# Moving four stages of a hand-ordered attention block to other slots

## The chip, the cores and the metric

The kernel runs on one core of one Trainium2 chip. The metric is the time of one execution on the device in microseconds (us). The engines are TensorE (PE, with its weight loads PEld), VectorE (DVE), ScalarE (ACT), GpSimd (POOL) and SyncE (SP), which only issues DMAs here. Each engine works through its own queue in order; semaphores tie the queues together.

## What is computed

The input x is 4 x 4096 x 512 in float32. Three residual steps follow each other: half an FFN, neighbourhood attention, half the same FFN again.

```python
x = x + 0.5 * ffn(layernorm(x))
x = x + attention(layernorm(x))
x = x + 0.5 * ffn(layernorm(x))
```

The FFN is one 512 x 512 product with a bias. Its input and its weight are first quantised in blocks of 32 values to a 6-bit grid, each block with a scale of its own (largest magnitude over 7.5). The attention has 16 heads of 32 features; each query sees 13 neighbouring keys (its window is shifted at the ends of the sequence), gets a bias by relative position, and goes through softmax, the weighted sum of the values, and an output product.

## The kernel before

The 16384 rows are 128 tiles of 128 rows; four tiles are a group. Attention works on items: item m is one group and one of four chunks of 128 features (4 heads), so there are 128 items too. Every float32 operand of a product is split into two float16 parts, high and low, and a product of a tile is 12 matmuls of 128 x 512 (three pairs of parts, four chunks), written by `product` (L144). High parts are made on ACT, low parts on DVE (L193 and L197 for the norms).

The work is cut into stages, Python generators that are hung up on a line of slots by hand. `begin(slot, stage, rank)` hangs a stage up; `run_slot` runs what hangs there, lowest rank first, each up to its next `yield n, rank`, and hangs it up again n slots later. The order in which the program is written down this way is the order on every engine; no scheduler changes it. Seven slots (`STEP`) are one step, and each step takes one tile t and one item m further in every stage. The names below are those of the profile.

- `load` (L169) fetches tile t into x.
- `moments` (L173, L174, DVE) takes mean and variance; `quantised_norms` then makes the quantised input of an FFN, at most two tiles at a time, the first norm of tile t+15 (n1) together with the third norm of tile t (n3): factors rsq, nbq on POOL (L179 to L188), normalise yq on ACT (L226), block maxima sc and their reciprocals on DVE (L232, L233, L237), scale on POOL (L239), round to 8 bits on ACT (L242), scale back on POOL (L244), high and low parts hlq (L193, L197), and a DMA transpose into xT.
- `first_half`: product pmf (f1), sum into x on DVE (L272), the second norm of the tile (rsn, yn, hln), and a transpose into x2.
- `values`: product pmv, copied out by ACT (L307) and DVE (L308), stored to DRAM; `load_stack` brings it back, three shifted copies under each other (vs).
- `project_qk`: two products pmqk (q and k), copied out by ACT (L379) and DVE (L383), q spread over two interleaved copies by ACT (L390).
- `softmax`: small matmuls for the scores ps (L458); on DVE the bias table and the second half of the sums (L500, L503) and the maxima top (L507); POOL subtracts (L509); ACT takes the exponentials (L511); DVE sums and inverts (L514 to L516); POOL multiplies (L518); ACT and POOL make the parts of p (L522, L523, L525); a DMA transposes p into pT (L527).
- `attend`: small matmuls pv (L549; pw for an 18th block of queries), copied to a ring by ACT (L576) and DVE (L582).
- `project_out`: product pmo from the ring, sum into x on DVE (L595), and at once the moments of n3.
- `second_half`: product pmf again (f2), sum into x (L272), store to DRAM (L601).
- `add_bias` adds a bias to x on POOL (L610), three times for each tile.

The slots come from the constants of L607: tile t runs f1 at 7t+5, v at 7t+20, out at 7t+93 and f2 twelve later; item m runs q and k from 7m+38, scores from 7m+42, values at 7m+59. Modulo 7 this gives the order of a step. The last tiles (`LAST`, `HELD`, `out_slot`, `second_slot`) have slots of their own. PSUM has three buffers for all products of a tile (`ps_m`), one for scores and one for values, so a product waits until the one that had its buffer is copied out.

Of the kernel before, what the change touches and what calls it, by code (L numbers as in the profile page):

```python
# [63 lines left out]
def macaron_kernel(  # L64
# [67 lines left out]
    def bc(t, n):  # L132

        return t.unsqueeze(2).to_broadcast([t.shape[0], t.shape[1], n])
# [4 lines left out]
    def product(pm, lhs, rhs):  # L139

        n = 0
        for a, b in ((0, 1), (1, 0), (0, 0)):
            for c in range(KC):
                nc.tensor.matmul(  # L144
                    pm, lhs(a, c), rhs(b, c), start=(n == 0), stop=(n == 3 * KC - 1)
                )
                n += 1
# [7 lines left out]
    def begin(slot, stage, rank=5):  # L155
        slots.setdefault(slot, []).append((rank, stage))
# [159 lines left out]
    def span(j):  # L316

        q0 = min(j * QN, length - QN)
        return q0, min(max(q0 - NS, 0), length - KN)

    def kind(j):
        return 1 if j == 0 else 2 if j == n_blocks - 1 else 0

    def late(j):

        return QR - QN if j == n_blocks - 1 else 0
# [11 lines left out]
    def straight(n):  # L338

        return -(-n // 2)  # L340
# [5 lines left out]
    n_items = n_batch * NG * KC  # L346
    qk, probs, stacks = {}, {}, {}

    def item_of(m):

        g, c = divmod(m, KC)
        return g // NG, g % NG, c
# [88 lines left out]
    def softmax(m):  # L441

        b, g, c = item_of(m)
        j0, j1 = group_blocks[g]
        n = j1 - j0
        tq, tk = qk.pop(m)
        ps = ps_s.tile([P, 2, 2, 2, 256], F32, tag="s", name=f"ps{m}")
        half = straight(n)
        for a in range(half):
            for part, sides in ((0, 2), (1, 1)):  # L450
                for i in range(a, n, half):
                    q0, k0 = (KN + at - g * GT for at in span(j0 + i))
                    q0 -= late(j0 + i)
                    u, w = divmod(a, PSB)
                    for r in (0, 2 * D):
                        rows = slice(r, r + 2 * D)
                        o = r if i < half else 2 * D - r
                        nc.tensor.matmul(  # L458
                            ps[o : o + 2 * D, i // half, u, :sides, w * KN : (w + 1) * KN],
                            tq[rows, part, 2 * q0 : 2 * (q0 + QR)],  # L460
                            tk[rows, :sides, k0 : k0 + KN],
                            start=part == 0, stop=part == 1,
                        )

        yield 1, 9
        sf = sfp.tile([P, MAXB, KN], F32, tag="sf", name=f"sf{m}")

        both = sf[:, : 2 * half, :].rearrange("p (v w) k -> p v w k", v=2)

        def parts(special):  # L470

            for w, e in ((0, PSB), (PSB, half)):
                lone = [(v, x) for v, x in special if w <= x < e]
                for v, x in lone:
                    yield slice(v, v + 1), slice(x, x + 1), 2 + v
                two = min(e, n - half)
                w0 = w + (1 if (0, w) in lone else 0)
                two -= 1 if (1, two - 1) in lone else 0
                if w0 < two:
                    yield slice(0, 2), slice(w0, two), 0  # L480
                for v, x, y in ((0, two, e), (1, w, w0)):
                    y = min(y, (half, n - half)[v])
                    if x < y and not (v == 0 and (v, x) in lone):
                        yield slice(v, v + 1), slice(x, y), v

        def sums(v, w, side):

            u, x = divmod(w.start, PSB)
            t = ps[:, v, u, side, x * KN : (x + w.stop - w.start) * KN]
            return t.rearrange("p v (w k) -> p v w k", k=KN)  # L490

        special = []
        if kind(j0) == 1:
            special.append((0, 0))
        if kind(j1 - 1) == 2:
            special.append((1, n - half - 1))
        for v, w, k in parts(special):
            o = both[:, v, w, :]
            bias = table[:, k : k + v.stop - v.start, c, :].unsqueeze(2).to_broadcast(o.shape)
            nc.vector.tensor_tensor(o, sums(v, w, 0), bias, ALU.add)  # L500
        for v, w, _ in parts([]):
            o = both[:, v, w, :]
            nc.vector.tensor_tensor(o, o, sums(v, w, 1), ALU.add)  # L503
        yield 1, 2
        s = sf[:, :n, :]
        top = sm.tile([P, MAXB], F32, tag="top", name=f"top{m}")
        nc.vector.tensor_reduce(top[:, :n], s, AX.X, ALU.max)  # L507
        yield 1, 4
        nc.gpsimd.tensor_tensor(s, s, bc(top[:, :n], KN), ALU.subtract)  # L509
        yield 1, 9  # L510
        nc.scalar.activation(s, s, AF.Exp, scale=alpha)  # L511
        yield 1, 4
        total = sm.tile([P, MAXB], F32, tag="total", name=f"total{m}")
        nc.vector.tensor_reduce(total[:, :n], s, AX.X, ALU.add)  # L514
        nc.vector.reciprocal(total[:, :n], total[:, :n])
        nc.vector.tensor_tensor(total[:, :n], total[:, :n], p_scale[:, :n], ALU.mult)  # L516
        yield 1, 4
        nc.gpsimd.tensor_tensor(s, s, bc(total[:, :n], KN), ALU.mult)  # L518
        yield 2, 8
        p = p_tile  # L520
        ph = p[:, :n, :KN]
        nc.scalar.copy(ph, s)  # L522
        nc.scalar.copy(p[:, :n, 2 * KN : KV], ph)  # L523
        yield 2, 4
        nc.gpsimd.tensor_tensor(p[:, :n, KN : 2 * KN], s, ph, ALU.subtract)  # L525
        pT = ptp.tile([P, MAXB, P], F16, tag="pT", name=f"pT{m}")
        nc.sync.dma_start_transpose(out=pT[:, :n, :], in_=p[:, :n, :].rearrange("p n k -> p (n k)"))  # L527
        probs[m] = pT
# [58 lines left out]
    def project_out(t, slot):  # L587

        r = t * P % RING
        pm = ps_m.tile([P, dim], F32, tag="mm", name=f"pmo_{t}")  # L590
        product(
            pm, lambda s, c: ring[:, s, c, r : r + P], lambda s, c: wt[:, s, c, PO : PO + dim]
        )
        yield 1, 8
        nc.vector.scalar_tensor_tensor(xs[t], pm, cp, xs[t], ALU.mult, ALU.add)  # L595
        moments(slot, t, "n3")

    def second_half(t):

        yield from ffn(t, "f2")  # L600
        nc.sync.dma_start(out=of[t * P : (t + 1) * P, :], in_=xs.pop(t))  # L601


    EARLY = 3
    STEP = 7

    F1, V, QK, SC, PV, OUT, F2 = 5, 2 * STEP + 6, 5 * STEP + 3, 6 * STEP, 8 * STEP + 3, 13 * STEP + 2, 12  # L607

    def add_bias(t, b):
        nc.gpsimd.tensor_tensor(xs[t], xs[t], b, ALU.add)  # L610
# [8 lines left out]
    HELD = range(NT - 15, NT - 7)  # L619
    LAST = NT - GROUP - 1  # L620

    def out_slot(t):


        i = t - LAST
        if i >= 0:
            return (n_items - 1) * STEP + PV + 3 + 2 * i
        if i >= 1 - GROUP:
            return LAST * STEP + PV + 21 + 4 * i
        return t * STEP + OUT  # L630

    def second_slot(t):

        i = t - LAST
        if t in HELD:
            return (n_items - 1) * STEP + PV - (16, 13, 10, 6, 5, 4, 3, 2)[t - HELD[0]]
        if i in (-2, -1):
            return out_slot(NT - 1) + 3 + i
        return out_slot(t) + F2

    for t in range(NT):
        k = t * STEP
        sooner = (0, 2, 5, STEP)[t] if t <= EARLY else 0
        begin(k - 18 - (STEP if t == EARLY else 0), one(load, t), 0)
        slot = k - 10 - (10 if t == EARLY else 0)
        enlist(slot, t, "n1")
        if not 0 < t < EARLY:
            begin(slot - 1, one(moments, slot, t, "n1"), 1)
        begin(k + F1 - sooner, first_half(t))
        begin(k + V, values(t))  # L650
        begin(k + F1 - sooner, one(add_bias, t, half_ffn_b), 8)
        at = out_slot(t)
        begin(at - 5, one(add_bias, t, after_b), 8)
        enlist(at + 2, t, "n3")
        begin(at, project_out(t, at + 2))
        begin(at + 6 if t < LAST else second_slot(t) - 2, one(add_bias, t, half_ffn_b), 8)
        begin(second_slot(t), second_half(t))
    for slot in together:
        if together[slot][0][0][1] == "n3" or together[slot][0][0][0] >= EARLY:
            begin(slot, quantised_norms(slot), 1)  # L660
    for m in range(n_items):
        k = m * STEP
        begin(k + QK, project_qk(m))
        begin(k + SC, softmax(m), 6)
        begin(k + PV, attend(m), 6)
    for n in range(n_batch * NG):
        k = n * GROUP * STEP
        b, g = divmod(n, NG)
# [4 lines left out]
    with tc.tile_pool(name="setup", bufs=1) as sp, tc.tile_pool(name="scratch", bufs=2) as scr:  # L673
# [23 lines left out]
        for o in chunks:  # L697
            w, i = (qkv_w, o) if o < 3 * KC else (proj_w, o - 3 * KC)
# [145 lines left out]
        for turned in (0, 2):  # L844
            for h in range(4):
                at = row_of(h ^ turned)
# [41 lines left out]
        slot = first  # L888
# [49 lines left out]
```

## Time and profile before

| what | value |
|---|---|
| median of three runs | 2293.57 us (2292.76 to 2294.65) |
| the profiled execution | 2295.28 us, its span 2293.5 us |
| PE busy | 2214.2 us, 97% of the span |
| PE weight loads busy | 1052.9 us, 46% |
| DVE busy | 2011.7 us, 88% |
| POOL busy | 1969.2 us, 86% |
| ACT busy | 1695.5 us, 74% |
| mean granted clock of TensorE | 0.993 |
| chain that ended last: share of PE | 87% |
| chain: share of DVE, ACT, POOL, DMA | 7%, 2%, 2%, 1% |

The span goes from the first instruction's start to the last one's end. A busy time is the sum of an engine's instructions; waiting for a semaphore does not count. The timeline gives for each instruction its start from the beginning of the span, its length, the line of the kernel, and what it writes and reads; in brackets stands idle time of the engine before it and what ended that.

### The profile page before, as it was taken

The numbers are of one execution on the slowest core, as the hardware profiler recorded it, in microseconds if no ns is written. First come the engines' busy times: TensorE is split into PE (matmuls) and PEld (weight loads), VectorE is DVE, ScalarE is ACT, GpSimd is POOL, SyncE is SP. The second block draws the span as 40 slices with busy tenths as digits, with TensorE's granted clock in tenths as the row PEclk, the third lists the DMA queues.
The fourth block names the chain that finished last, engine by engine and source line by source line (L and its number), as shares of the span: only waits on it lengthen the run. The fifth ranks groups of instructions, "written<-read, shape, count | busy, mean of one in ns | idle before, by whom it ended". The sixth has DMA issues, their size and how long they took to land.

```text
span 2293.5 us, 65425 instructions
## 1 busy us (share of the span) xinstructions
PE 2214.2 (97%) x26771; PEld 1052.9 (46%) x26771; DVE 2011.7 (88%) x3769; ACT 1695.5 (74%) x2544; POOL 1969.2 (86%) x2006
## 2 busy tenths in 40 slices
PE   3799999999999999999999999999999999999978
PEld 1344444444444444444444444444444444444433
DVE  6899998888988988898988998888988988989775
ACT  5697777777777777777777777777777777777752
POOL 4588988988988988888888888888888889888776
PEclk9999999999999999999999999999999999999989
DMA  7687776777767777777776776777776777866654
GB/s 201 153 178 161 162 160 154 159 162 158 160 156 155 164 162 154 161 158 157 162 158 155 162 161 154 160 157 155 164 160 151 167 158 154 166 155 147 137 107 104
DMA packets 926213, 359.61 MB, mean 157 GB/s; under 512 B 719452, under 2 KB 890328, under 8 KB 925912
## 3 DMA queue, kind: packets, MB, share of 16 engines
q1 hardware_dynamic: 925568, 354.90, 70.8%
q8 instruction: 209, 3.42, 0.6%
q14 instruction: 92, 0.75, 0.1%
q10 hardware_dynamic: 344, 0.53, 0.1%
HBM read 110.26 MB, written 67.29 MB: 77 GB/s over the span
## 4 chain that ended last, share of the span: by engine, by line
PE 87%; DVE 7%; ACT 2%; POOL 2%; DMA 1%; issue 1%; SPq 0%; ACTq 0%; DVEq 0%; POOLq 0%
PE pmqk L144 27%; PE pmf L144 26%; PE pmo L144 14%; PE pmv L144 13%; PE ps L458 4%; PE pv L549 3%; DVE stn L173 1%; DVE hlq L197 1%; DVE hln L197 1%; DVE sc L232 1%; ACT qk L390 0%; DVE x L272 0%; POOL yq L239 0%; DVE total L514 0%; DVE qf L383 0%
## 5 line engine op out<-in xcount | busy, mean ns | idle before, releaser
L144 PE MATMUL pmf<-wt,xT 128*128 128x512 f16 x3048 | 702.7, 381 | 13.3 <-DMA xT<-hlq 7.4
L144 PE MATMUL pmqk<-x,wt 128*128 128x512 f16 x3072 | 705.8, 379 | 0.4 <-DVE after_b L836 0.4
L144 PEld LDWEIGHTS <-xT 128*128 128x128 f16 x3048 | 298.4, 98 | 377.2 <-DMA xT<-hlq 15.2
L144 PEld LDWEIGHTS <-wt 128*128 128x128 f16 x3072 | 289.7, 98 | 336.0 <-issue 1.3
L239 POOL TENSOR_TENSOR yq<-yq,r 128x1024 f32<-128x1024 f32 (+1 forms) x141 | 247.1, 1752 | 135.6 <-DVE r L237 124.1
L144 PE MATMUL pmv<-wt,x 128*128 128x512 f16 x1536 | 353.9, 380 | 4.2 <-DVE qf L383 2.6
L144 PE MATMUL pmo<-wt,ring 128*128 128x512 f16 x1536 | 357.2, 383 | 0.0
L390 ACT ACTIVATE qk<-qf,parity 128x1024 f16<-128x1024 f16 x256 | 349.3, 1432 | 0.0
L610 POOL TENSOR_TENSOR x<-x,half_ffn_b 128x512 f32<-128x512 f32 x256 | 327.8, 1281 | 0.0
L272 DVE SCALAR_TENSOR_TENSOR x<-pmf,coef,x 128x512 f32<-128x512 f32 x256 | 180.0, 703 | 144.7 <-PE pmf L144 141.1
L576 ACT ACTIVATE ring<-pv 128x510 f16<-128x510 f32 (+7 forms) x176 | 78.7, 475 | 307.3 <-PE pv L549 234.4
L173 DVE BATCH_NORM_STATS2 stn<-x 128x6 f32<-128x512 f32 x384 | 265.2, 691 | 8.8 <-DMA x<-in_L_attn_x_dram 0.2
L244 POOL TENSOR_TENSOR yq<-q,sc 128x1024 f32<-128x1024 fp8e4 (+1 forms) x141 | 246.2, 1746 | 4.8 <-ACT q L242 4.8
L144 PEld LDWEIGHTS <-x 128*128 128x128 f16 x1536 | 150.5, 98 | 186.9 <-issue 4.9
L242 ACT ACTIVATE q<-yq,nudge 128x1024 fp8e4<-128x1024 f32 (+1 forms) x141 | 150.0, 1064 | 115.9 <-POOL yq L239 107.6
L144 PEld LDWEIGHTS <-ring 128*128 128x128 f16 x1536 | 141.2, 98 | 160.5 <-issue 5.0
L518 POOL TENSOR_TENSOR sf<-sf,total 128x714 f32<-128x714 f32 (+2 forms) x128 | 178.7, 1396 | 37.2 <-DVE total L516 19.3
L226 ACT ACTIVATE yq<-x,nbq,rsq 128x512 f32<-128x512 f32 x254 | 193.1, 803 | 16.7 <-POOL nbq L185 15.2
L525 POOL TENSOR_TENSOR p<-sf,p 128x714 f16<-128x714 f32 (+2 forms) x128 | 192.5, 1504 | 0.0
L509 POOL TENSOR_TENSOR sf<-sf,top 128x714 f32<-128x714 f32 (+2 forms) x128 | 182.4, 1425 | 3.5 <-DVE top L507 3.3
L197 DVE TENSOR_TENSOR hlq<-yq,hlq 128x1024 f16<-128x1024 f32 (+1 forms) x141 | 167.6, 1189 | 8.7 <-ACT hlq L193 6.6
L610 POOL TENSOR_TENSOR x<-x,after_b 128x512 f32<-128x512 f32 x128 | 162.9, 1274 | 0.0
(143 smaller groups left out, 3441.0 us busy)
## 6 DMA issues: line engine op xcount, KB each, us to landing
vs<-vd SPq DMA_DIRECT2D x144, 357.0 KB
x<-in_L_attn_x_dram SPq DMA_DIRECT2D x128, 256.0 KB
vd<-vt SPq DMA_DIRECT2D x128, 256.0 KB
out_dram<-x SPq DMA_DIRECT2D x128, 256.0 KB
vs<-vd SPq DMA_DIRECT2D x24, 378.0 KB
vs<-vd SPq DMA_DIRECT2D x24, 315.0 KB
rows<-in_L_attn_qkv_w_dram SPq DMA_DIRECT2D x12, 256.0 KB
xT<-hlq SPq DMA_TRANSPOSE x141
```

Source lines behind the costliest of these rows:

```text
L144: nc.tensor.matmul(pm, lhs(a, c), rhs(b, c), start=(n == 0), stop=(n == 3 * KC - 1))
L173: nc.vector.bn_stats(st, xs[t])
L197: nc.vector.tensor_tensor(hl[:, :, 1, :], y, hl[:, :, 0, :], ALU.subtract)
L226: nc.scalar.activation(y[:, u], xs[t], AF.Identity, bias=nb[:, u : u + 1], scale=rs[:, u : u + 1])
L239: nc.gpsimd.tensor_tensor(yb, yb, bc(r, QB), ALU.mult)
L244: nc.gpsimd.tensor_tensor(yb, q8.rearrange("p u (n q) -> p (u n) q", q=QB), bc(sc, QB), ALU.mult)
L272: nc.vector.scalar_tensor_tensor(xs[t], pm, cf, xs[t], ALU.mult, ALU.add)
L390: nc.scalar.activation(to, whole[0], AF.Copy, scale=parity[:, e : e + 1])
L509: nc.gpsimd.tensor_tensor(s, s, bc(top[:, :n], KN), ALU.subtract)
L518: nc.gpsimd.tensor_tensor(s, s, bc(total[:, :n], KN), ALU.mult)
L525: nc.gpsimd.tensor_tensor(p[:, :n, KN : 2 * KN], s, ph, ALU.subtract)
L610: nc.gpsimd.tensor_tensor(xs[t], xs[t], b, ALU.add)
```

## The change

The constants and ranks move these stages: `attend` four slots later (7m+63, behind the scores of item m+3 in the same slot), except that the last three items keep 7m+59; `project_out` two slots later (7t+95) and the joint norms with it (n1 from 7t-10 to 7t-8 for tiles after `EARLY`, n3 still two slots behind the out-projection); f2 at fourteen slots behind the out-projection and so four later (7t+109); softmax's sums on DVE and all of softmax behind them one slot later. `LAST_PV` keeps the slots of the last tiles' out-projections and second FFNs. In the ranks, out-projection goes behind the second FFN and that behind k in their common slot. No instruction is added or removed.

```diff
@@ softmax
         nc.scalar.activation(s, s, AF.Exp, scale=alpha)
-        yield 1, 4
+        yield 2, 4
         total = sm.tile([P, MAXB], F32, tag="total", name=f"total{m}")
@@
-    F1, V, QK, SC, PV, OUT, F2 = 5, 2 * STEP + 6, 5 * STEP + 3, 6 * STEP, 8 * STEP + 3, 13 * STEP + 2, 12
+    F1, V, QK, SC, PV, OUT, F2 = 5, 2 * STEP + 6, 5 * STEP + 3, 6 * STEP, 9 * STEP, 13 * STEP + 4, 14
+
+    LAST_PV = (n_items - 1) * STEP + 8 * STEP + 3
@@ out_slot
-            return (n_items - 1) * STEP + PV + 3 + 2 * i
+            return LAST_PV + 3 + 2 * i
         if i >= 1 - GROUP:
-            return LAST * STEP + PV + 21 + 4 * i
+            return LAST * STEP + 82 + 4 * i
         return t * STEP + OUT
@@ second_slot
         if t in HELD:
-            return (n_items - 1) * STEP + PV - (16, 13, 10, 6, 5, 4, 3, 2)[t - HELD[0]]
+            return LAST_PV - (16, 13, 10, 6, 5, 4, 3, 2)[t - HELD[0]]
         if i in (-2, -1):
             return out_slot(NT - 1) + 3 + i
-        return out_slot(t) + F2
+        return out_slot(t) + (F2 if t < LAST else 12)
@@
-        slot = k - 10 - (10 if t == EARLY else 0)
+        slot = k - (8 if t > EARLY else 20 if t == EARLY else 10)
@@
-        begin(at, project_out(t, at + 2))
+        begin(at, project_out(t, at + 2), 7)
         begin(at + 6 if t < LAST else second_slot(t) - 2, one(add_bias, t, half_ffn_b), 8)
-        begin(second_slot(t), second_half(t))
+        begin(second_slot(t), second_half(t), 6)
@@
-        begin(k + PV, attend(m), 6)
+        begin(k + (PV if m < n_items - 3 else PV - 4), attend(m), 7)
```

## What was predicted

> **What bounds the kernel now.** I began with the busy shares in 40 slices, to see which engine is full and where.
>
> ```profile
> PE   3799999999999999999999999999999999999978
> DVE  6899998888988988898988998888988988989775
> POOL 4588988988988988888888888888888889888776
> ```
>
> TensorE (PE) is in the top class from the third slice nearly to the end; VectorE (DVE) and GpSimd (POOL) sit at 8 to 9 tenths, so they have 10 to 15% to give away and no more. A table of 100 us stretches says how full PE is; from 300 to 2100 us all eighteen rows read 100.00, as here:
>
> ```profile
> 1000.00:1100.00 100.00, 100.00 (x1242) 47.85 (x1240) 89.57 (x166) 76.58 (x114) 89.22 (x88) 1.00 0.72 157
> ```
>
> The columns after the stretch are its length, then the busy us of PE, weight load, DVE, ScalarE (ACT) and POOL, then the granted clock: PE 100, DVE 89.6, ACT 76.6, POOL 89.2, clock 1.00. Next, the timeline of PE for one step (start, length, what):
>
> ```profile
> 1000.80 0.81 PE L458 MATMUL ps<-qk 64*64 64x84 f16 x68
> 1001.53 2.76 PE L144 MATMUL pmo<-wt,ring 128*128 128x512 f16 x12
> 1004.14 2.75 PE L144 MATMUL pmqk<-x,wt 128*128 128x512 f16 x12
> 1006.82 0.69 PE L549 MATMUL pv<-pT,vs 126*32 126x30 f16 x68
> 1007.45 2.76 PE L144 MATMUL pmqk<-x,wt 128*128 128x512 f16 x12
> 1010.04 2.75 PE L144 MATMUL pmf<-wt,xT 128*128 128x512 f16 x12
> 1012.63 2.75 PE L144 MATMUL pmv<-wt,x 128*128 128x512 f16 x12
> ```
>
> The next scores (ps) start at 1017.91, so a step lasts 17.11 to 17.12 us and PE sets it. A product of 12 matmuls starts 2.59 to 2.60 us after the one ahead when that is a product too (1010.04, 1012.63), but a small block starts 2.68 us after the product ahead of it (1004.14 to 1006.82): entering each small block costs 0.08 to 0.09 us. Everything else hides behind PE as long as it keeps the step.
>
> **What the change does to the queues.** I read the order on each engine from the changed program.
>
> *PE.* The order q, k, second FFN (f2), out-projection, first FFN (f1), v, scores, values replaces f2, scores, out, q, values, k, f1, v. No matmul is added. The values now follow the scores directly, so one of two entries from a product is gone (0.085 us) and one from block to block is new; the trace has none such. Bounds: it costs nothing (0.085 won) or as much as the old entry (0 won). I take the middle, 0.04: both blocks have small tiles, but of different shape. PE's own need becomes 17.04 to 17.12. The Trainium skill ("TensorEngine Tiling (Array Packing)", Key Properties) says that a switch of tiling mode drains TensorE; by that the new entry costs like the old one, and nothing is won.
>
> *DVE.* A step holds the same 24 kinds of operations. Start to start in the timeline of 1000 to 1018 us: q low part L383 0.67, the norms' L173 and L174 three times 0.73+0.10, f2 and f1 sums L272 0.70+0.68, out sum L595 0.76, k low L383 0.66, L197 of hlq 1.12, L514 0.92, L515 0.30, L516 0.10 when nothing is in its way (at 165.15), L308 0.60, L232 1.24, L233 0.23, L237 0.27, L500 0.95, L503 1.05, L582 0.60, L507 0.82, L197 of hln 0.60. Sum 14.8 us. That fits 17.05.
>
> *New waits around PE.* PSUM buffers change hands: the out product now takes the buffer of q, so PE waits for L383 of q. On DVE everything from the out sum round to the next L383 of q stands in front of that wait: 14.8 less the three items between (0.73+0.10+0.70) is 13.2; with 2.79 from the product's start to its sum (the last pmf starts at 1000.49, L272 at 1000.90) the circle is 16.1 us. It closes inside 17.05 with 0.9 to spare. f1 takes the buffer of f2 and v that of out; at PE's pace those sums end 1.7 us before they are needed and nothing stands in front of them on DVE.
>
> *DMAs and SP.* No transfer is added. hlq's transpose had 7.17 us from L197's end (1008.06) to its product (1015.23), and in the steady part no product waited for it; the new order gives 8.2 us at PE's pace and 7.1 at my forecast pace, nothing. Its turn on SP is behind the out store, which waits only for L272 of f2, done four us earlier. The p transpose is issued one slot later and read four later: nothing. The stack loads keep their slots; the last reader of the same buffer moves from 8 slots ahead to 4, some 10 us, so SP is not held. x tiles live four slots longer, of 161 that 23 buffers give: nothing.
>
> *ACT.* It is busy 76.6 of 100; its low rank work moves, and it comes in below as a link.
>
> **Where it goes wrong: POOL and DVE stop each other.** The reader should see this in two places of the old trace.
>
> ```profile
> 202.18 1.42 DVE L197 TENSOR_TENSOR hlq<-yq,hlq 128x1024 f16<-128x1024 f32 x1 [0.25 <-ACT hlq L193]
> 203.53 1.94 DVE L197 TENSOR_TENSOR hln<-yn,hln 128x512 f16<-128x512 f32 x1
> ...
> 201.03 1.49 POOL L525 TENSOR_TENSOR p<-sf,p 128x714 f16<-128x714 f32 x1
> 202.49 2.43 POOL L509 TENSOR_TENSOR sf<-sf,top 128x756 f32<-128x756 f32 x1
> ```
>
> POOL's L509 takes 1.39 to 1.46 us elsewhere. Here it began under DVE's L197 and ended 1.32 us after that one's end (203.60). The L197 of hln, 0.68 us elsewhere, ended 0.55 us after L509. So one waits for the whole of the other. In the steady step it is the same, but cheap:
>
> ```profile
> 1005.48 1.39 POOL L509 TENSOR_TENSOR sf<-sf,top 128x714 f32<-128x714 f32 x1
> ...
> 1006.86 1.20 DVE L197 TENSOR_TENSOR hlq<-yq,hlq 128x1024 f16<-128x1024 f32 x1
> 1007.03 1.08 POOL L179 TENSOR_SCALAR rsq<-mv 128x2 f32<-128x2 f32 x1 [0.16 <-DVE mv L174]
> ...
> 1011.01 1.27 POOL L610 TENSOR_TENSOR x<-x,half_ffn_b 128x512 f32<-128x512 f32 x1
> ...
> 1011.41 0.91 DVE L516 TENSOR_TENSOR total<-total,p_scale 128x17 f32<-128x17 f32 x1
> ```
>
> L179 lasts 0.19 alone (1016.86) and 1.08 under L197; L516 0.18 alone and 0.91 behind L610. Only L197 and L516 show it; L272, L595 and L383, which read PSUM, do not. The Trainium skill ("SBUF — State Buffer", Who interferes with whom) has the rule: a DVE instruction with two SBUF inputs and a GpSimd instruction that reads SBUF exclude each other, and whichever issues second fully blocks. It adds no number to the sum.
>
> Take the new step at PE's pace, q's start as 0. The out sum comes at 7.78+2.79 = 10.57; behind it L173, L174 and L383 of k, so L197 of hlq is asked at 10.57+0.76+0.73+0.10+0.66 = 12.8. On POOL the order is L509, half_ffn_b add, L244, L525, half_ffn_b add, the four small ones of the joint norm, after_b add. The top (L507) would end at about 6.4, and L509 follows: 1.40+1.24+1.87+1.46 later, at 12.4, the second add begins and runs to 13.6. **They collide**: L197 would wait some 0.8. Moreover L197 of hln now follows L507 directly and is asked 0.1 us ahead of L509, so L509 waits 0.5 for it and the add comes at 12.9; then it waits for L197. Either order loses about a microsecond, because a circle runs through both:
>
> L507 0.90, POOL L509 1.40, add 1.24, L244 1.87, L525 1.46, add 1.36 (1.27 and the 0.08 gap ahead of a small one), L179 0.27, L182 0.67, L187 0.28, L188 0.23: 9.68. ACT: two norms L226 0.71+0.80 (they now stand in front of L307, which DVE's L308 needs), L307 0.58: 2.09. DVE: L308 0.60, L232 1.24, L233 0.23, L237 0.27, L500 0.95, L503 1.05, L582 0.60, back to L507: 4.94. Together 16.7, and 0.2 for hand-overs of 0.03 to 0.14 each: **16.9 without blocking**, only 0.15 inside PE's pace. Blocking adds 0.5 at L509 and 0.75 where L179 waits behind L197 (L197 ends 1.08 after the add, less what L179 would have taken): **18.15 us**. In the order before, the small ones of the joint norm followed L509 at once (1005.48, 1007.03), so the circle was shorter by three long POOL operations, 4.6 us, and hlq's L197 met only the small L179.
>
> **Sum.** f2 runs with tiles 0 to 112 in the regular pattern, 113 steps; I take 111, the first two filling. 111 x (18.15 - 17.12) = 114 us. The ramp (nine steps without out and f2, 11 to 14 us long, DVE 97 busy of 100) may lose or win up to 5 us by the same collisions; the end keeps its slots by LAST_PV; both taken at 0. The profiled execution took 2295.28 us (span 2293.5), so 2409; the median of the runs is 1.7 lower, so **2408 us**.
>
> **Rivals.** (1) *PE keeps the pace.* For it: both circles close inside 17.05 unblocked, and DVE and POOL each have 1.5 us of idle time. It decides the other way as soon as blocking costs the circle less than 0.15 us a step. Its price is the entry alone, -0.04 (0 to -0.085) x 111: 2289 (2284 to 2294). Against: L509 behind hln's L197 is 0.5 already. (2) *Half the blocking*: hlq's L197 falls beside L187 or L188 and only the 0.5 remains: 17.4, +0.3 x 111 = 2327 (2315 to 2350). (3) *More blocking*: L516 also falls behind the after_b add (0.8 us as at 1011.41), or the 128-deep transposes become late; 18.5 to 18.7: 2445 to 2470. (4) That the change does not do what it says is excluded: the order on PE is in the program.
>
> **How the numbers follow.** Forecast 0.65 (2375 to 2430), half 0.14, more 0.06, PE's pace 0.15. A measurement here tells 0.2% (4.6 us) from no change. Rival 1 is faster by more than that in about half its cases. Slower 0.85, same 0.07, faster 0.08. The range runs from 2322, inside the half case, to 2460, inside the third, leaving out rival 1 and the edges: about 0.18.
>
> **What would show it.** The step from ps to ps at 18.1; idle time on PE of about 1 us a step ahead of the out product, put down to DVE L383; L509 near 1.9; L197 of hlq near 2.2 or the half_ffn_b add above 2; L308 waiting for ACT L307. If L197 stays at 1.2, L509 at 1.4 and PE at 100, I am wrong and rival 1 holds; if only L509 is long, rival 2.

## The result, and the profile after

The changed kernel takes **2507.86 us** (median of four runs, 2506.25 to 2513.07) beside 2293.23 us for the kernel before (four runs, 2292.76 to 2294.65): a ratio of **1.0938, 95% interval 1.0924 to 1.0952**. Slower, as forecast; but the forecast was 2408 and its range ended at 2460. Of the 215 us lost, 115 were foreseen.

Its page, the profiled run (span 2504.8 us): the busy times, the slices of PE, DVE and POOL, and the chain that ended last. In the changed kernel's profile lines behind L606 stand two further down, so the biases' L610 is L612.

```profile
PE 2260.2 (90%) x26771; PEld 1068.8 (43%) x26771; DVE 1968.4 (79%) x3769; ACT 1698.3 (68%) x2544; POOL 1960.1 (78%) x2006
...
PE   3888999999999999999999999999999999999978
...
DVE  6887788777878788778877777877878878878776
...
POOL 4677887878888887778887788788788778888766
...
POOL 26%; DVE 24%; PE 22%; DMA 17%; issue 9%; ACT 3%; POOLq 0%; DVEq 0%; SPq 0%; ACTq 0%
DMA xT<-hlq 16%; PE pmf L144 10%; PE pmo L144 7%; POOL x L612 6%; POOL yq L244 5%; POOL sf L509 4%; POOL p L525 3%; DVE stn L173 3%; DVE sc L232 3%; PE pmqk L144 3%; POOL yq L239 3%; DVE hlq L197 2%; POOL rsq L179 2%; DVE vt L308 2%; POOL rsq L182 2%
```

No engine is full any more: DVE fell from 88 to 79%, POOL from 86 to 78%. The chain was PE for 87%; now it goes round POOL, DVE and PE, and 16% of it is one transfer, hlq's transpose. What PE waits for says it outright (us in total, times, longest):

```profile
PE pmf L144 <- DMA xT<-hlq: 128.5, 57, 5.1
...
PE pmqk L144 <- issue: 16.0, 13, 2.9
```

The wait that the prediction named, the out-projection for DVE's L383 of q, is not there at all. Here is PE through one late step and the next:

```profile
1011.49 0.81 PE L458 MATMUL ps<-qk 64*64 64x84 f16 x68
1012.22 0.69 PE L549 MATMUL pv<-pT,vs 126*32 126x30 f16 x68
1012.85 4.27 PE L144 MATMUL pmqk<-x,wt 128*128 128x512 f16 x19
1018.65 1.25 PE L144 MATMUL pmqk<-x,wt 128*128 128x512 f16 x5 [1.53 <-issue]
1021.75 5.30 PE L144 MATMUL pmf<-wt,xT 128*128 128x512 f16 x12 [1.84 <-DMA xT<-hlq]
1026.85 3.15 PE L144 MATMUL pmo<-wt,ring 128*128 128x512 f16 x12
1029.83 2.75 PE L144 MATMUL pmf<-wt,xT 128*128 128x512 f16 x12
1032.42 2.75 PE L144 MATMUL pmv<-wt,x 128*128 128x512 f16 x12
1035.10 0.81 PE L458 MATMUL ps<-qk 64*64 64x84 f16 x68
```

From scores to scores it is 23.6 us here; the next step takes 17.0 (1035.10 to 1052.11), the one after 21.5. Long and short alternate. In the long one f2 waits for its transposed input, and then its 12 matmuls take 5.30 us instead of 2.75: the clock was granted at half.

Now SP, which issues the DMAs (start, time to issue). First the kernel before, two steps:

```profile
1005.55 1.72 SPq L527 DMA_TRANSPOSE pT<-p  x1
1008.09 2.53 SPq L198 DMA_TRANSPOSE xT<-hlq  x1
...
1012.03 0.56 SPq L433 DMA_DIRECT2D vs<-vd  x1
...
1025.20 1.58 SPq L198 DMA_TRANSPOSE xT<-hlq  x1
...
1029.23 1.06 SPq L433 DMA_DIRECT2D vs<-vd  x2
```

And the changed kernel, the late step and the next:

```profile
1008.60 1.64 SPq L527 DMA_TRANSPOSE pT<-p  x1
1010.29 1.19 SPq L433 DMA_DIRECT2D vs<-vd  x2
1011.59 0.43 SPq L601 DMA_DIRECT2D out_dram<-x  x1
1012.11 6.75 SPq L198 DMA_TRANSPOSE xT<-hlq  x1
...
1028.31 0.56 SPq L433 DMA_DIRECT2D vs<-vd  x1
1028.97 0.51 SPq L601 DMA_DIRECT2D out_dram<-x  x1
1033.59 1.61 SPq L198 DMA_TRANSPOSE xT<-hlq  x1
```

Before, hlq's transpose goes out ahead of the stack loads (L433: two in one step, one in the next). After, it stands behind them, and behind two of them its issue takes 6.75 us. Its input was ready at 1010.90 (L197 below, start plus length), it went out at 1012.11, SP was done with it at 1018.86, and f2 began at 1021.75; PE had wanted it at 12.85 + 5.19, that is 1018.04. The reason is in the slots. A tile's transpose hung at 7t+102, which is 4 modulo 7, with a low rank; the loads hang at 4 modulo 7 too (7 x 6 + 4 and so on) with rank 9, behind it. The joint norms moved two slots on, the transpose to 7t+104, which is 6 modulo 7, and the loads stayed.

The predicted collisions are there too, in the timeline of DVE and POOL of the changed kernel at the same place:

```profile
1008.54 1.27 POOL L612 TENSOR_TENSOR x<-x,half_ffn_b 128x512 f32<-128x512 f32 x1
1008.73 2.17 DVE L197 TENSOR_TENSOR hlq<-yq,hlq 128x1024 f16<-128x1024 f32 x1
1009.90 1.05 POOL L179 TENSOR_SCALAR rsq<-mv 128x2 f32<-128x2 f32 x1
```

L197 (1.20 before) waits inside its own 2.17 us for the add, and L179, 0.19 alone, for L197. This step is the worst: in the changed kernel L197 takes over 1.5 us in 43 of the 106 steps counted below. So two things delay the kernel, and the question for the experiments is what each is worth.

For all kernels below, the starts of the scores' rows on PE were counted into three parts: the start of the 13th item's scores, the mean of the 106 steps from there to the 119th, and the rest of the span.

| kernel | time, us | 13th scores at | mean step | rest |
|---|---|---|---|---|
| before | 2295.28 | 264.6 | 17.122 | 214.0 |
| after | 2506.66 | 281.8 | 18.806 | 229.5 |
| a1, loads behind hlq's transpose | 2400.73 | 273.3 | 17.956 | 222.3 |
| a5, loads on ACT's queue | 2401.53 | 276.2 | 17.943 | 221.1 |
| a2, adds out of the circle | 2426.49 | 284.0 | 18.096 | 222.5 |
| a3, a1 and a2 | 2323.24 | 274.8 | 17.241 | 219.2 |
| a4, a3 and p's copies behind q's | 2297.93 | 269.6 | 17.081 | 216.0 |
| a6, a4 with the old ramp | 2293.00 | 263.0 | 17.071 | 218.7 |
| b1, before with the loads ahead | 2401.18 | 279.8 | 17.949 | 217.1 |
| b2, before with the values moved | 2315.64 | 265.9 | 17.245 | 220.0 |
| b3, before with the sums moved | 2331.05 | 268.9 | 17.380 | 218.1 |

Each time in it is that of the profiled run; the medians of a4 and a6 stand with them. a1 to a6 start from the changed kernel, b1 to b3 from the one before. Two theories stand against each other. Theory Q: SP's queue delays hlq's transpose, since it now stands behind the stack loads. The rival: the prediction's circle, in which DVE and POOL stop each other, is the loss, and the late transposes are its consequence. If Q alone holds, the loads undo the loss; if the rival alone, the adds do.

### The profile page after: what moved, and what is told of

Its sections match the earlier page's. It is cut to its first block, busy times and chain, and to the rows that moved or that the text cites. A ratio compares the mean times of both kernels' runs of the same rounds, so it can differ in the third digit from the quotient of the medians.

```text
span 2504.8 us, 65717 instructions
## 1 busy us (share of the span) xinstructions
PE 2260.2 (90%) x26771; PEld 1068.8 (43%) x26771; DVE 1968.4 (79%) x3769; ACT 1698.3 (68%) x2544; POOL 1960.1 (78%) x2006
## 4 chain that ended last, share of the span: by engine, by line
POOL 26%; DVE 24%; PE 22%; DMA 17%; issue 9%; ACT 3%; POOLq 0%; DVEq 0%; SPq 0%; ACTq 0%
DMA xT<-hlq 16%; PE pmf L144 10%; PE pmo L144 7%; POOL x L612 6%; POOL yq L244 5%; POOL sf L509 4%; POOL p L525 3%; DVE stn L173 3%; DVE sc L232 3%; PE pmqk L144 3%; POOL yq L239 3%; DVE hlq L197 2%; POOL rsq L179 2%; DVE vt L308 2%; POOL rsq L182 2%
## 5 line engine op out<-in xcount | busy, mean ns | idle before, releaser
L144 PE MATMUL pmf<-wt,xT 128*128 128x512 f16 x3048 | 741.8, 396 | 146.9 <-DMA xT<-hlq 128.5
L144 PE MATMUL pmqk<-x,wt 128*128 128x512 f16 x3072 | 695.2, 382 | 16.1 <-issue 16.0
L509 POOL TENSOR_TENSOR sf<-sf,top 128x714 f32<-128x714 f32 (+2 forms) x128 | 224.7, 1755 | 171.9 <-DVE top L507 171.9
L239 POOL TENSOR_TENSOR yq<-yq,r 128x1024 f32<-128x1024 f32 (+1 forms) x141 | 248.1, 1760 | 131.6 <-DVE r L237 127.0
L612 POOL TENSOR_TENSOR x<-x,half_ffn_b 128x512 f32<-128x512 f32 x256 | 331.3, 1294 | 0.0
L272 DVE SCALAR_TENSOR_TENSOR x<-pmf,coef,x 128x512 f32<-128x512 f32 x256 | 189.9, 742 | 147.2 <-PE pmf L144 143.1
L595 DVE SCALAR_TENSOR_TENSOR x<-pmo,coef,x 128x512 f32<-128x512 f32 x128 | 95.9, 749 | 236.8 <-PE pmo L144 226.2
L193 ACT CAST hlq<-yq 128x1024 f16<-128x1024 f32 (+1 forms) x141 | 135.3, 959 | 202.9 <-POOL yq L244 192.4
L144 PEld LDWEIGHTS <-ring 128*128 128x128 f16 x1536 | 151.1, 99 | 186.6 <-issue 8.8
L197 DVE TENSOR_TENSOR hlq<-yq,hlq 128x1024 f16<-128x1024 f32 (+1 forms) x141 | 188.5, 1337 | 9.8 <-ACT hlq L193 8.8
L511 ACT ACTIVATE sf<-sf,coef 128x714 f32<-128x714 f32 (+2 forms) x128 | 114.7, 896 | 111.5 <-POOL sf L509 111.5
```

The lines of the kernel that those rows point to most:

```text
L144: nc.tensor.matmul(pm, lhs(a, c), rhs(b, c), start=(n == 0), stop=(n == 3 * KC - 1))
L197: nc.vector.tensor_tensor(hl[:, :, 1, :], y, hl[:, :, 0, :], ALU.subtract)
L239: nc.gpsimd.tensor_tensor(yb, yb, bc(r, QB), ALU.mult)
L272: nc.vector.scalar_tensor_tensor(xs[t], pm, cf, xs[t], ALU.mult, ALU.add)
```

## The experiments

### a1: the stack loads behind hlq's transpose

```diff
+        o = 2 if n < n_batch * NG - 1 else 0
-        begin(k + 6 * STEP + 4, load_stack(b, g, 0), 9)
-        begin(k + 8 * STEP + 4, load_stack(b, g, 1), 9)
+        begin(k + 6 * STEP + 4 + o, load_stack(b, g, 0), 9)
+        begin(k + 8 * STEP + 4 + o, load_stack(b, g, 1), 9)
```

> The kernel after, with the loads of the value stacks two slots later, so that SP issues them behind hlq's transpose instead of in front of it (the last group keeps its slots). Theory Q (queue): in the kernel after, hlq's transpose is issued behind one or two stack loads, lands late in every second step, the second FFN's product waits for it and then runs at half clock; that is 128 us of PE waiting on xT, some 45 us of half clock and the idle time called issue. Under Q alone nothing of it is left: 2295 to 2310 us, steps of 17.0 to 17.2. Theory C (circle, as predicted): VectorE and GpSimd block each other, 18.15 us a step whatever the DMAs do: about 2408 us, every step alike. Both together: 2400 to 2410, with no wait on xT.

Measured: **2400.73 us**, 107 less than after. SP again issues the transpose first:

```profile
1295.72 0.53 SPq L601 DMA_DIRECT2D out_dram<-x  x1
1296.34 2.14 SPq L198 DMA_TRANSPOSE xT<-hlq  x1
1298.58 1.16 SPq L433 DMA_DIRECT2D vs<-vd  x2
```

The steps no longer alternate: 93 of 106 take 17.5 to 18.4, the median 17.9. And the wait that was forecast appears in the list of what PE waits for:

```profile
PE pmo L144 <- DVE qf L383: 51.6, 74, 1.7
...
PE pmf L144 <- DMA xT<-hlq: 13.5, 5, 5.1
```

The timeline of POOL in the same kernel:

```profile
1293.93 1.27 POOL L612 TENSOR_TENSOR x<-x,half_ffn_b 128x512 f32<-128x512 f32 x1
1295.29 1.05 POOL L179 TENSOR_SCALAR rsq<-mv 128x2 f32<-128x2 f32 x1
...
1305.47 1.77 POOL L509 TENSOR_TENSOR sf<-sf,top 128x714 f32<-128x714 f32 x1 [1.20 <-DVE top L507]
```

This is the circle of the prediction: L509 at 1.77 instead of 1.40 behind L197 of hln (1305.30, 0.68), L179 at 1.05 instead of 0.19 behind L197 of hlq (1294.31, 1.98). L197 of hlq takes over 1.5 us in 100 of the 106 steps (mean 1.90). A second wait, which the prediction did not name, is that of an FFN product for DVE's L582 (20.5 us, 25 times); L582 lies on the same circle. One undone order among the DMAs turns the changed kernel into the one that was forecast.

### b1: the kernel before with only the loads ahead

```diff
-                yield STEP, 9
+                yield STEP, 0
...
-        begin(k + 6 * STEP + 4, load_stack(b, g, 0), 9)
-        begin(k + 8 * STEP + 4, load_stack(b, g, 1), 9)
+        begin(k + 6 * STEP + 4, load_stack(b, g, 0), 0)
+        begin(k + 8 * STEP + 4, load_stack(b, g, 1), 0)
```

> The kernel before, with the same loads given the first rank of their slot, so that they stand in front of hlq's transpose as they do in the kernel after. Nothing else moves. Theory Q: with two loads in front the transpose needs about 9.6 us (as in the kernel after) where there are 7.2 until the second FFN's product; 2.4 us late in every second step and about 1 us of half clock: 2430 to 2490 us, alternating steps. Theory C: no change, 2293 us.

Measured: **2401.18 us**. Nothing but the turn of the loads on SP changed, and 106 us are lost, less than Q expected. The rows are those of after:

```profile
1294.93 1.16 SPq L433 DMA_DIRECT2D vs<-vd  x2
1296.18 5.65 SPq L198 DMA_TRANSPOSE xT<-hlq  x1
...
1312.25 0.56 SPq L433 DMA_DIRECT2D vs<-vd  x1
1313.81 3.01 SPq L198 DMA_TRANSPOSE xT<-hlq  x1
```

PE waits 80.6 us for xT, 55 times, and long and short steps alternate. Theory C, which expected no change, is out. PE's waits are shorter than in after (at most 2.6 us in the 106 steps, against 4.1), and less of the clock is lost: 20 us at half clock in the 106 steps, against 82 in after.

### a5: the loads on another engine's queue

```diff
-                nc.sync.dma_start(
+                nc.scalar.dma_start(
```

> The kernel after, with the stack loads issued by ScalarE's own DMA queue in the same place of the order; the same bytes at about the same time on the same 16 DMA engines, but no longer in front of hlq's transpose on SP's queue. If the transpose is late because it stands behind the loads in one queue (Q): no wait on xT, and the circle alone is left, 2395 to 2415 us as in the first kernel of this study. If it is late because the loads take the DMA engines' time: alternating steps and 2480 to 2520 us as in the kernel after.

Measured: **2401.53 us**, the same as a1 within 1 us. The loads move the same bytes, but not, as was expected, at about the same time: they go out from ACT's queue a median 7.9 us (7.0 to 8.8) behind hlq's transpose. So a5 takes them from in front of it, as a1 does, and its time alone does not tell the queue from the transfers. hlq's transpose takes its old time, and the loads now stand 1.5 us (median) ahead of hln's transpose, in another queue:

```profile
1298.80 2.18 SPq L198 DMA_TRANSPOSE xT<-hlq  x1
...
1306.78 0.31 ACTq L433 DMA_DIRECT2D vs<-vd  x1
...
1308.48 1.24 SPq L198 DMA_TRANSPOSE x<-hln  x1
```

The issue of hln's transpose takes its usual 1.24 us (median of the 106 steps; longest 1.87), although packets of the loads are still moving when it ends, in all 106. In SP's own queue it is otherwise. Packets of the transposes are 256 bytes long, those of the loads 512, those of the out store 2048. This is what moved in the late step of after, in the first 4.5 us of the transpose's issue and from there to 1019.0:

```profile
DMA packets 1421, 0.79 MB, mean 176 GB/s; under 512 B 93, under 2 KB 1368, under 8 KB 1420
...
DMA packets 716, 0.32 MB, mean 133 GB/s; under 512 B 621, under 2 KB 640, under 8 KB 716
```

First the loads and the store, then the transpose. In after the issue ends 0.2 to 0.5 us after the last packet of these in 90 of 106 steps, in b1 in 80. By these rows the transpose is held by its place in SP's queue, for as long as the transfers ahead of it there take. One comparison is missing: hln's transpose is half as large as hlq's, and in no run do the loads go out ahead of hlq's from another queue. The Trainium skill ("DMA: Bandwidth & Descriptors", Issuing engines are not separate DMA queues) says that starting DMAs from several engines only saves the sequencer the time to initiate them, "which is usually small relative to the DMA itself". What its place in SP's queue costs a transpose here is not small: the issue of hlq's transpose takes 5.6 us with two loads or more ahead of it in after (median of 65 steps) and 2.2 in before.

### a2 and a3: the adds out of the circle

```diff
-        begin(k + F1 - sooner, one(add_bias, t, half_ffn_b), 8)
+        begin(k + F1 + 1 - sooner, one(add_bias, t, half_ffn_b), 2)
...
-        begin(at + 6 if t < LAST else second_slot(t) - 2, one(add_bias, t, half_ffn_b), 8)
+        begin(at + (12 if t < HELD[0] else 6) if t < LAST else second_slot(t) - 2, one(add_bias, t, half_ffn_b), 8)
```

a2 has this edit, a3 this and a1's.

> The kernel after, with the two half_ffn_b adds of GpSimd taken out from between L509 and the joint norm's small ones (one behind them, one behind L239), which shortens the circle by 2.5 us and leaves L197 of hlq nothing long to collide with. Theory C: back to PE's pace, 2290 to 2300 us, L197 of hlq at 1.2 us. Theory Q: the stack loads still stand in front of the transpose; it is asked up to 1 us earlier in every second step, so 2450 to 2508 us, steps still alternating, PE still waiting 75 to 128 us on xT.

> Both edits, stack loads behind the transpose and adds out of the circle. If Q and C are all there is: PE's pace of 17.05 us a step, 2283 to 2297 us, no wait on xT, L197 at 1.2. A third cause would leave it above 2320 us.

Measured: a2 **2426.49 us**, 24 under Q's range and far above C's, and PE still waits for xT (78.2 us, 50 times); a3 **2323.24 us**, with steps of 17.24. Taking away the circle wins 81 us, the queue 107, both 185: nearly the sum. But a3 is 26 us above its expectation, in the range that was to show a third cause. Its out-projections start 2.80 us after f2 instead of 2.59, and ACT shows why:

```profile
1297.02 0.79 ACT L522 CAST p<-sf 128x714 f16<-128x714 f32 x1
1297.83 0.79 ACT L523 COPY p<-p 128x714 f16<-128x714 f16 x1
1298.53 1.14 ACT L242 ACTIVATE q<-yq,nudge 128x1024 fp8e4<-128x1024 f32 x1
1299.58 0.67 ACT L379 ACTIVATE qf<-pmqk,qk_b 128x512 f16<-128x512 f32 x1
```

PE has q done at about 1295.7 (1293.09 and 2.60), but ACT copies it (L379) only after p's two copies and L242, at 1299.58, and DVE's L383 reads what L379 wrote. That L383 frees the PSUM buffer that the out product at 1301.08 takes.

### a4: p's copies behind q's

```diff
-        yield 2, 8
+        yield 4, 6
         p = p_tile
...
-        yield 2, 4
+        yield 1, 4
         nc.gpsimd.tensor_tensor(p[:, :n, KN : 2 * KN], s, ph, ALU.subtract)
```

It also leaves the first adds of tiles 0 to 15 where they were.

> The third kernel (stack loads behind the transpose, adds out of the circle) with two more moves: ACT's two copies of p come behind the copy of q (and GpSimd's low part of p one slot later), and the first-FFN add of the first 16 tiles stays where it was. In the third kernel a step lasts 17.21 us though PE needs 17.00; the trace shows ACT's L379 of q queued behind the p copies and L242, VectorE's L383 of q behind that, and the out product 0.2 us behind L383. If that chain is the whole remainder, the step becomes 17.00: 0.11 below the kernel before over 111 steps, minus 12 us, against some 8 us lost in the ramp and the end: 2285 to 2297 us. If another wait stands behind it, 17.1 to 17.2 and 2300 to 2320 us.

Measured: **2298.37 us** (median of ten runs, 2297.66 to 2300.3), ratio 1.0023, interval 1.0014 to 1.0033, 1.4 us above its expectation. The wait is gone, and the median step is 17.01. The mean is 17.08, since ten of the 106 steps take 17.3 to 17.8, and why is open; and what the ramp and the end lose (5.0 and 2.0 us) is more than the 4.3 us that the 106 steps win.

### b2 and b3: one move alone, in the kernel before

b2 moves only the values (PV as in the change), b3 only softmax's sums:

```diff
-        yield 1, 4
+        yield 2, 4
         total = sm.tile([P, MAXB], F32, tag="total", name=f"total{m}")
```

> The kernel before, with the values moved behind the scores of the item three ahead and nothing else. GpSimd's order and the transposes are those of the kernel before, so neither Q nor C costs anything. The scores and the values stand together, which saves 0.11 us a step (2600 and 2590 instead of 2683 ns for a product in front of a block, and two 10 ns starts), but the out-projection follows two places behind the values: every fourth one needs the ring rows that they have just written and waits some 2 us for ACT's L576 and VectorE's L582. 2293 - 12 + 28 x 2 = 2330 to 2345 us.

> The kernel before, with softmax's sums and all behind them one slot later and nothing else. GpSimd's low part of p then stands behind the joint norm's small ones, and p's transpose behind those of hlq and hln on SP. Both theories: the stack loads stay behind hlq's transpose and no long GpSimd operation comes into the path from the maxima to the joint norm, so no change: 2288 to 2300 us.

Measured: b2 **2315.64 us**, 14 below its expectation: most steps take 17.01, but about every fourth 17.5 to 17.7 (15 times the out product waits for DVE's L582, 4.7 us) and a few 18 to 21. In its 106 steps PE's waits put down to "issue" are longer (9 times at the values, 8.4 us). b3 **2331.05 us**: the expectation failed, a loss of 38 us from one slot. The sums now stand on DVE behind L237, just when POOL multiplies by what L237 gave:

```profile
1222.05 1.91 POOL L239 TENSOR_TENSOR yq<-yq,r 128x1024 f32<-128x1024 f32 x1 [0.58 <-DVE r L237]
...
1222.94 1.05 DVE L516 TENSOR_TENSOR total<-total,p_scale 128x16 f32<-128x16 f32 x1
1223.91 0.74 DVE L272 SCALAR_TENSOR_TENSOR x<-pmf,coef,x 128x512 f32<-128x512 f32 x1
```

L516, 0.18 alone, takes 1.05 and ends with L239; L272 behind it is late, and PE's out product waits for it 43 times (12.4 us in all). But L516 is nearly as long in before (mean of the 106 steps 0.87, here 1.00), where k's L383 stands behind it. What is new is L233, which takes 0.19 in before and 1.12 here on the mean, behind POOL's adds. So DVE is blocked for about 1 us a step more, most of it at L233; which part of the 38 us comes from it and which from L516's new place is not shown.

### a6: a4 with the ramp of the kernel before

```diff
-        yield 2, 4
+        ramp = m < 8
+        yield 1 if ramp else 2, 4
...
-        slot = k - (8 if t > EARLY else 20 if t == EARLY else 10)
+        slot = k - (8 if t >= 15 else 20 if t == EARLY else 10)
...
-        begin(k + (PV if m < n_items - 3 else PV - 4), attend(m), 7)
+        begin(k + (PV if 8 <= m < n_items - 3 else PV - 4), attend(m), 7 if m >= 8 else 6)
...
-        o = 2 if n < n_batch * NG - 1 else 0
+        o = 2 if 2 <= n < n_batch * NG - 1 else 0
```

p's copies too keep their old slots for items 0 to 7.

> The kernel of a4_p_behind_q with the ramp left as in the kernel before: for items 0 to 7 the sums and the values keep their old slots, the joint norms shift only from tile 15 on, and the stack loads are two slots later only from the third group on. Nothing of the reference is left out. Theory Q with the small collisions (the changed order is worth 0.11 us a step once the loads, the adds and the copies of p stand right; the ramp's 5.7 us that a4_p_behind_q lost by item 20 come only from its changed slots there): 2298.4 - 5.7, so 2290 to 2295, and scores to scores 17.00 in the steady part. Rival: the ramp is lost wherever the regime starts, because the pipeline has to be refilled at the switch: 2296 to 2300, unchanged.

Measured: **2290.50 us** (median of 11 runs, 2289.36 to 2293.06) beside 2293.38 (15 runs) for the kernel before: ratio **0.9989, interval 0.9980 to 0.9998**. That is 2.9 us, at the bound of what can be told from no change, and within its expectation. PE in it:

```profile
1002.97 2.75 PE L144 MATMUL pmf<-wt,xT 128*128 128x512 f16 x12
1005.56 2.75 PE L144 MATMUL pmo<-wt,ring 128*128 128x512 f16 x12
...
1010.74 2.75 PE L144 MATMUL pmv<-wt,x 128*128 128x512 f16 x12
1013.42 0.81 PE L458 MATMUL ps<-qk 64*64 64x84 f16 x68
```

With q and k ahead of these rows and f1 left out, all products at 2.59 and one entry, 1010.74 to 1013.42, at 2.68: the order that the change wanted, with no wait in it. The median step is 17.01, the mean 17.07. In the profiled runs the 106 steps are 5.4 us shorter than before's and the ramp 1.6, the end 4.7 longer.

## Where the prediction was right and where it failed

- **PE bounds the kernel, and the entry is worth little: right, slightly mis-sized.** I took 0.04 us a step, between 0 and 0.085. a4 and a6 show 17.00 to 17.01 against 17.11: 0.11. These are median steps; the means win only 0.04 and 0.05. From the scores' start to what follows it is 0.74 us before (a full product) and after (the values), so the values behind the scores cost no more to enter than a product there, and the one entry saved is 0.093 (2.683 less 2.590); the other 0.01 is products that took 2.60 and now take 2.59. By the page on tiling that the prediction quoted the new entry would have cost like the old one; it did not. Whether something drains at each of these changes, before and after, the trace does not tell.
- **PSUM buffers and the DVE–PE circle: it closes, as worked out.** But only when q's copy on ACT is early. The prediction called ACT "a link" and costed its moves at nothing; in a3 p's copies ahead of L379 cost 0.2 us in the median step. From a3 to a4 it is 25 us, 17 of them in the 106 steps; that edit also left 16 adds unmoved.
- **DMAs and SP: this step failed.** "Its turn on SP is behind the out store, which waits only for L272" looked at one neighbour. The stack loads keep their slots, and hlq's transpose was moved past them; the text asks whether the loads would be held, and not whom they hold. Then "7.1 at my forecast pace, nothing" took 7.1 us from L197 to the product as ample. What it must hold was not asked: with one load ahead of it in SP's queue the transpose takes 3.6 us to issue in after (40 steps), with two or more 5.6 (65 steps), against 2.2 before. In b1, in the 51 steps in which f2 comes after idle time, it starts 8.7 us after L197's end (median) where before had 7.2; in after it is 10.1 (55 steps). Undoing the order alone (after to a1) wins 107 us. Rival 3 names it ("or the 128-deep transposes become late") with 0.06 and 0.35 to 0.55 us a step beside the circle; it was 0.85 (18.81 less 17.96).
- **The circle through POOL and DVE: right.** a1, which has it alone, takes 2401 where 2408 was forecast. The step is 17.96 and not 18.15, so 0.83 x 106 = 88 us; L509 lost 0.37 and not 0.5, L179 0.78 (1.05 less the 0.27 of its turn in the sum) where 0.75 was worked out. That the total fits nonetheless is in part luck: it comes from the ramp and the end, taken at 0, which lose 8.7 and 8.3 us. Moving the adds out of it (a1 to a3) wins 77 us.
- **The two together.** In after the ramp loses 17.2 us, the 106 steps 178.6 and the end 15.5. a1's steps alone lose 88.4 and b1's 87.7, which add up to 176.1. That is close to 178.6, but no proof that the two are independent: in after no out product waits for L383 (a late f2 may give DVE and POOL time to catch up; this was not tested), and up to 41 us of the loss is the clock, 82 us at half of it.
- **What would show it.** L509 near 1.9 (1.755 on the mean) and L308 waiting for L307 (40.3 us) came. L197 near 2.2 came in part: 2.17 in the step shown, but over 2 in 3 of 106 steps in after and in 31 in a1. A step of 18.1 and the idle before the out product did not come in after, and both came in a1 (17.9).

What remains open: why SP holds a transpose until the transfers ahead of it have moved, and whether it would hold another kind of DMA so. What PE's "issue" waits (16.0 us) are is not in the trace. The joint norms' and projections' move alone, without that of the values, was not tried.

## What to carry to other kernels

When a stage is moved, write down the whole order of the queue that issues its DMAs, with the transfers of every other stage, and ask of each pair that changes places whom it now holds up. A transfer's room is not only its time in flight: the issue itself can grow from 2 to 7 us with what is ahead of it in its queue. And a reordering that wins PE one entry of 0.1 us pays only once every cover it broke (SP's turn, POOL's circle, ACT's copies, the ramp) is laid again; each of those was worth 8 to 107 us here, the gain 11 at most (0.107 x 106).

## What the hardware showed unexpectedly

- **About 2 us of idle are enough for half the clock.** In the 106 steps of after, 21 times 3.41 or 6.83 us run at a clock of 0.5, and all these stretches begin a whole multiple of 3.413 us apart. In the 3.41 us ahead of each, PE had been idle between 1.98 and 3.14 us, once in two pieces (the stretch at 1020.8, behind the 1.53 and in the 1.84 above). Cut the 106 steps into windows of 3.41 us on the same grid: at full clock, every window with 2.02 us of idle or more was followed by half the clock, and of those with less only one, with 1.98; 13 with 1.71 (half a window) to 1.99 were not. In b1 the bound lies between 1.88 and 1.95, in a1 between 1.71 and 1.80. The Trainium skill ("TensorE: Matmul & The Clock Gate", What's actually happening) asks for an idle window of about 3.4 us; the length of the stretches agrees, the idle time needed does not.
- **A blocked instruction hides its wait in its own length.** L516 was 0.18 or 1.05, L179 0.19 or 1.05, L182 0.71 or 1.68 us, with no idle time shown ahead of them; L233 in b3 is a fourth (0.19 or 1.13). One looks for this by rows of one form with two lengths.
